# A paged-attention layer on one core: blocks exchanged directly from SBUF to SBUF, and new keys turned together with the first queries

## The chip, the core and the metric

The kernel runs on one core of a Trainium2 chip. The time is the device time of one execution in microseconds (us), as the median of several runs. The engines are TensorE (PE in the profile; its weight loads are listed as PEld), VectorE (DVE), ScalarE (ACT), GpSimd (POOL) and SyncE (SP), which here does nothing but issue transfers. Transfers are also issued from ScalarE's queue and from GpSimd's. All of them run on the core's 16 DMA engines.

## The reference

Eight sequences of 128 tokens with 512 features are first changed by a low-rank-adapter-like layer (one 512x512 matrix for each sequence, picked by a number), and then pass through one attention layer with a paged cache:

```python
x = x + einsum('bsi,boi->bso', x, weight[adapter_ids])
q, k, v = x @ Wq.T, x @ Wk.T, x @ Wv.T          # 32 query heads, 8 key heads of 128
q, k = rope(rmsnorm(q, q_norm_w), pos), rope(rmsnorm(k, k_norm_w), pos)
k_all = concatenate([k_cache[block_table], k])  # 512 cached keys, then 128 new ones
v_all = concatenate([v_cache[block_table], v])
scores = where(valid, q @ k_all.T / sqrt(128), -1e30)   # 4 query heads share a key head
x = x + (softmax(scores) @ v_all) @ Wo.T
```

Everything is float32.

## The kernel before, in words

The work is cut into 32 steps: four groups of key heads (two key heads and eight query heads each) times eight sequences. Step i works on the attention of its own group and sequence, on the projections of step i + 1, and on the value and output products of step i - 1. The steps 0 to 5 also compute the adapter layer of the later sequences.

A step has eight slots (h = 0 to 7), one for each block of scores: 128 rows by 640 keys. Four slots form a unit: the four query heads that share a key head (index j, 0 or 1), 32 tokens of each of the four heads in one slot. In a slot TensorE computes the scores (L1031), VectorE adds the mask and takes the minimum (L1041), ScalarE takes the exponential (L1057), VectorE the reciprocal of the sum (L1098), and GpSimd scales (L1105). Between two scores stand pieces of the other products (L559: `pj_kv`, `pj_q`, `o`, `out`), dealt out over the slots in the order of the list `main` so that each slot gets an equal share. The program writes out the order by hand; `pending`, `later`, `to_write` and `to_read` are lists of work that is emitted one slot later.

Three kinds of blocks have to be turned, with tokens or features brought onto the partitions: probabilities, cached keys and queries. VectorE turns them within blocks of 32 x 32 (`tp`, L871; `tk`, L786; `tq`, L807). What is left is an exchange of whole rows between partitions. The kernel before does this by way of DRAM, on SP's queue: one transfer writes the turned tile to a DRAM tile (`send`, `send_k`, `send_q`: L889, L791, L809), and a second one, which waits for the first, reads it back in the other order (`receive`, `receive_k`, `receive` in `send_q`: L898, L799, L816).

New keys (`k`, from the projection of step i + 1) are turned by TensorE instead: `turn_k` multiplies by the identity (L763) and ScalarE copies the result from PSUM into the last 128 columns of `kT` (L764). For that, `rotate` has GpSimd write the keys in a different order of their columns (`turned_order`, L671). `turn_k(i + 1, 0)` is placed in slot 6 of step i and `turn_k(i, 1)` in slot 2 of step i. At the ends of the program (the set `by_pe`: both query halves of step 0, the first of step 1, both of the last step) queries are turned by TensorE as well.

The weights of the next group are loaded, turned by VectorE, written to DRAM and read back in the same manner, on ScalarE's queue. Cached keys and values are gathered by GpSimd.

Buffers: `tk`, `tq0`, `tq1`, `kT0`, `kT1`, `qT0`, `qT1`, `q0`, `q1` and `k` have one buffer each, `tp` has two, `pT` one in each of two pools. The scores have two PSUM buffers, everything else four.

Of the kernel before, what the change touches and what calls it, by code (L numbers as in the profile page):

```python
# [18 lines left out]
P = 128  # L19
# [33 lines left out]
def lora_then_paged_attention(  # L53
# [173 lines left out]
    )  # L227
    mhalf = const.tile([P, GQ + GK], FP, name="mhalf")
    nc.gpsimd.memset(mhalf, -0.5)
    masks = [const.tile([P, 4, NC, Q4], FP, name=f"mask_{n}") for n in range(2)]  # L230
    for m in masks:
        nc.gpsimd.memset(m[:, :, LC, :], 0.0)


    lora_ix = const.tile([P, B], I32, name="lora_ix")
# [12 lines left out]

    steps = [(g, b) for g in range(G) for b in range(B)]
    last = len(steps) - 1  # L250
    TR = 0.11
    turns_at = {}

# [3 lines left out]
    for i, (g, b) in enumerate(steps):  # L257
        if i == 0:
            at(i, 2, False, lambda: turn_q(0, 1))
            at(i, 7, False, lambda: turn_q(1, 0))  # L260
            for n, h in enumerate((7, 8, 9, 10)):
                at(i, h, False, lambda n=n: turn_weights(("o1", 0, n)))
        if i == last:
            at(i - 1, 6, False, lambda: turn_q(last, 0))
            at(i, 2, True, lambda: turn_q(last, 1))
        at(i, 2, True, lambda i=i: turn_k(i, 1), 1)
        if i < last:
            at(i, 6, False, lambda i=i: turn_k(i + 1, 0), 1)
        if g == 0 and b + 2 < B:
            at(i, 0, True, lambda b=b: turn_x(b + 2))  # L270
            for c in range(KC):
                at(i, c if i else c + 2, False, lambda b=b, c=c: turn_lora(b + 2, c))
            at(i, 8 if i else 9, True, lambda b=b: turn_x1(b + 2))
    for turns in turns_at.values():
        turns.sort(key=lambda t: not t[0])

# [111 lines left out]
    def rope_angles():  # L388
        nc.vector.tensor_copy(row_f[:, 0:B], row_i[:, 0:B])
        row = spread(0)  # L390
        nc.vector.tensor_copy(len_f, row[:, 0:B])
        par_f = rope["par"] = const.tile([P, 1], FP, name="par_f")
        nc.vector.tensor_copy(par_f, par)
        pos = const.tile([P, B], FP, name="pos")
        nc.vector.tensor_scalar(pos, len_f, par_f, None, ALU.add)
        def temp(tag):
            t = work.tile([P, 4, D], FP, tag=tag, name=f"rope_{tag}")
            return t.rearrange("p h (u d) -> p (h u) d", u=2)
# [14 lines left out]
        nc.vector.tensor_scalar(ang, ang, PI_BELOW, -PI_BELOW, ALU.min, ALU.max)  # L413
        rope.update(ang=ang, sin=sin, cos=cos)
# [213 lines left out]

    def make_mask(i):

        b = steps[i][1]
        nc.vector.tensor_scalar(
            masks[i % 2][:, :, 0:LC, :], key_no, len_f[:, b : b + 1], FAR, ALU.is_ge, ALU.mult
        )


    by_pe = {(0, 0), (0, 1), (1, 0), (last, 0), (last, 1)}

    def rotate(i, y, dst, ss, table, n, between=None):

# [8 lines left out]
        sw = work.tile([P, 4, D], FP, tag="sw", name=f"sw_{i}_{table}")  # L649


        turned_order = i > 0 and (table == 1 or (i, n) in by_pe)
        cw = dst
        if turned_order and table:
            cw = sw[:, 2 : 2 + heads, :]
        elif turned_order:
            cw = work.tile([P, 4, D], FP, tag=f"tq{n}", name=f"cw_{i}_{n}")
# [46 lines left out]
    def project(i, what):  # L704
# [1 line left out]
        s = st[i]  # L706

        def after_kv(y):
            s.k = work.tile([P, GK, D], FP, tag="k", name=f"k_{i}")
            s.vn = news.tile([P, GW], FP, tag="vn", name=f"vn_{i}")  # L710
            s.ss = [
                small.tile([P, 6], FP, tag=f"ss{n}", name=f"ss_{i}_{n}") for n in range(2)
            ]

            def rest():
                nc.scalar.copy(s.vn, y[:, GW : 2 * GW])
                rotate(i, y, s.k, s.ss[0][:, 4:6], 1, 0)

            pending.append(rest)

        def after_q(n):
            def after(y):
                s.q[n] = work.tile([P, 4, D], FP, tag=f"q{n}", name=f"q_{i}_{n}")

                def rest():
                    rotate(
                        i,
                        y,
                        s.q[n],
                        s.ss[n][:, 0:4],  # L730
                        0,
                        n,
# [26 lines left out]
    def turn_k(i, j, copy=None):  # L759
# [3 lines left out]
        nc.tensor.transpose(t.rearrange("d i a -> d (i a)"), s.k[:, j, :], ident)  # L763
        (copy or nc.scalar.copy)(s.kT[j][:, :, LC, :].rearrange("d a i -> d i a"), t)  # L764

    def turn_q(i, n, copy=None):
        s = st[i]
        assert n in s.scaled
        s.qT[n] = work.tile([P, 4, 4, Q4], FP, tag=f"qT{n}", name=f"qT_{i}_{n}")
# [3 lines left out]
        (copy or nc.scalar.copy)(  # L773
            s.qT[n].rearrange("d b h q -> d h b q"), t.rearrange("d (h b q) -> d h b q", h=4, b=4)
        )


# [1 line left out]

    to_read = []  # L780

    def send_k(i):
        s = st[i]
        tk = work.tile([P, 4, GK, LC * Q4], FP, tag="tk", name=f"tk_{i}")
        for j in range(GK):
            nc.vector.transpose(  # L786
                tk[:, :, j, :].rearrange("p a (c k) -> p a c k", c=LC),
                s.kc[:, :, j * D : (j + 1) * D].rearrange("p c (a d) -> p a c d", a=4),
            )
        s.xk = xch.tile([4, P, GK, LC * Q4], FP, tag="xk", name=f"xk_{i}")  # L790
        nc.sync.dma_start(  # L791
            out=s.xk.rearrange("b (i a) h x -> (b i) (a h x)", a=4),
            in_=tk.rearrange("p a h x -> p (a h x)"),
        )

    def receive_k(i, j):
        s = st[i]
        s.kT[j] = work.tile([P, 4, NC, Q4], FP, tag=f"kT{j}", name=f"kT_{i}_{j}")
        nc.sync.dma_start(  # L799
            out=s.kT[j][:, :, 0:LC, :].rearrange("d b c k -> d b (c k)"),  # L800
            in_=s.xk[:, :, j, :].rearrange("b d x -> d b x"),
        )

    def send_q(i, n):
        s = st[i]
        tq = work.tile([P, 4, 4, Q4], FP, tag=f"tq{n}", name=f"tq_{i}_{n}")
        nc.vector.transpose(tq, s.q[n].rearrange("p h (a d) -> p a h d", a=4))  # L807
        xq = xch.tile([4, P, 4, Q4], FP, tag=f"xq{n}", name=f"xq_{i}_{n}")
        nc.sync.dma_start(  # L809
            out=xq.rearrange("b (i a) h q -> (b i) (a h q)", a=4),  # L810
            in_=tq.rearrange("p a h q -> p (a h q)"),
        )

        def receive():
            s.qT[n] = work.tile([P, 4, 4, Q4], FP, tag=f"qT{n}", name=f"qT_{i}_{n}")
            nc.sync.dma_start(  # L816
                out=s.qT[n].rearrange("d b h q -> d b (h q)"),
                in_=xq.rearrange("b d h q -> d b (h q)"),
            )

        to_read.append((now[0], 0, receive))

    now = [0]

# [59 lines left out]
            t[:, 0:LA].rearrange("p (c b q) -> p c b q", c=NC, b=4),  # L884
        )

    def send(u):
        u.scr = xch.tile([4, P, REP * QK], FP, tag="xp", name=f"xp_{u.i}_{u.j}")
        nc.sync.dma_start(  # L889
            out=u.scr.rearrange("b (i a) x -> (b i) (a x)", a=4),  # L890
            in_=u.tp.rearrange("p a r k -> p (a r k)"),
        )

    def receive(u):

        pl, tag = (lora, "raw") if u.j and u.i >= B - 3 else (pts, "pT")
        pT = pl.tile([P, 4, REP, QK], FP, tag=tag, name=f"pT_{u.i}_{u.j}")
        nc.sync.dma_start(  # L898
            out=pT.rearrange("p b r k -> p b (r k)"), in_=u.scr.rearrange("b p x -> p b x")
        )  # L900
        st[u.i].pT[u.j] = pT

    def run(queue):
# [77 lines left out]
    for i, (g, b) in enumerate(steps):  # L981
# [38 lines left out]
        for h in range(8):  # L1020
# [9 lines left out]
            for lo, hi in ((0, L), (L, LA)):  # L1030
                nc.tensor.matmul(  # L1031
                    sc[:, lo:hi],
                    lhsT=s.qT[j][:, r, :, :].rearrange("d h q -> d (h q)"),
                    rhs=s.kT[j].rearrange("d a c i -> d (a c i)")[:, lo:hi],
                    start=True,
                    stop=True,
# [4 lines left out]
            nc.vector.tensor_tensor_reduce(  # L1041
                out=p,
                in0=sc[:, 0:LA],
                in1=masks[i % 2].rearrange("p a c i -> p (a c i)"),
                scale=1.0,
                scalar=3.0e38,
                op0=ALU.add,
# [12 lines left out]
            if prev is not None:  # L1060
# [1 line left out]
                if u.i < last or u.j == 0:  # L1062
                    turn_p(u, pr)
                if pr == REP - 1:
                    send(u)
                    to_read.append((8 * i + h, 1, lambda u=u: receive(u)))
            run(later)
            run(to_write)
            if 8 * i + h in turn_when:
# [6 lines left out]
            for _, _, f in sorted(due, key=lambda r: r[1]):  # L1076
                f()
            if h == 0 and i:
                receive_k(i, 1)
            if h == (1 if i else 3) and i < last:  # L1080
                send_k(i + 1)
            if h == 4 and i < last:
                receive_k(i + 1, 0)

            ahead = sum(c for k in range(h + 1, 8) for _, c, _ in turns_at.get((i, k), []))
            mine = sum(t[1] for t in turns)
# [96 lines left out]
```

## Time and profile before

| what | value |
|---|---|
| time, median of 3 runs | 1198.78 us (1196.74 to 1199.55) |
| profiled execution, its own time | 1197.03 us |
| its span | 1194.7 us |
| PE busy | 1178.0 us, 99% |
| VectorE, ScalarE, GpSimd busy | 61%, 44%, 56% |
| DMA: SP's queue (q1), ScalarE's (q10), GpSimd's (q0), share of 16 engines | 59.6%, 12.4%, 10.1% |
| HBM read, written | 195.04 MB, 132.12 MB |
| length of a step, steps 1 to 5 / 8 to 28 | 40.7 us / 34.6 us |

The lines of the profile read as follows. A group names the line of the kernel, the engine and the operation, then the tiles as output<-input, the shape, the count, the busy time and the mean duration, and after the last bar how long the engine was idle just before and for whom. A wait line has the waiting engine and tile, whom it waited for, the total in us, how many times, and the longest. A line of transfers has the queue that issues it (SPq, ACTq, POOLq), how many there were, the size of one, and the median time in us from issue to landing. The chain of waits is the sequence of work that ended last. The rows of slices cut the span in 40 equal parts, and a digit is the busy share in tenths. Float32 products show as two records per matrix product, and a matmul's duration overlaps with that of its neighbour, so the spacing of starts is the price of one.

### The profile page before, as it was taken

Reading aid. Unit: us, or ns where it says so; the run is one execution under the profiler, and the core shown is the slowest. Engines: PE = TensorE matmul, PEld = TensorE weight load, DVE = VectorE, ACT = ScalarE, POOL = GpSimd, SP = SyncE. Lnnn points to the kernel's source line nnn. Section 1 sums busy time; section 2 is a strip of 40 time slices with the busy share of each in tenths; the row PEclk is TensorE's granted clock in tenths of the full one; section 3 lists DMA queues with packets and bytes.
Section 4 is the critical chain, followed back from the end, with each engine's and each line's share of the span. In section 5 each row is a group of like instructions: output and inputs, shape, how many; then the busy total and the mean of one; then the engine's idle time right before and its main releaser. Section 6 shows DMA issues by size and latency. Waiting matters only on the chain.

```text
span 1194.7 us, 12971 instructions
## 1 busy us (share of the span) xinstructions
PE 1178.0 (99%) x3412; PEld 576.4 (48%) x3412; DVE 733.6 (61%) x1675; ACT 531.5 (44%) x1648; POOL 674.9 (56%) x781
## 2 busy tenths in 40 slices
PE   7899999999999999999999999999999999999998
PEld 4554455454444444444444444444444444444454
DVE  5566656665566666766566676666657655565651
ACT  4564444444444444444444444444444444444432
POOL 5566455545566556555655556565556556655540
PEclk9999999999999999999999999999999999999999
DMA  8388788877988988888998998888898987777761
GB/s 290 110 278 273 261 292 293 275 261 246 309 289 301 334 303 300 294 270 300 296 303 280 340 313 298 298 278 300 267 319 277 303 285 264 243 255 242 260 222 60
DMA packets 187148, 328.02 MB, mean 275 GB/s; under 512 B 13124, under 2 KB 106052, under 8 KB 178116
## 3 DMA queue, kind: packets, MB, share of 16 engines
q1 hardware_dynamic: 124272, 239.23, 59.6%
q10 hardware_dynamic: 49524, 48.12, 12.4%
q0 software_dynamic: 13280, 39.86, 10.1%
q8 instruction: 27, 0.44, 0.2%
q14 instruction: 45, 0.37, 0.1%
HBM read 195.04 MB, written 132.12 MB: 274 GB/s over the span
## 4 chain that ended last, share of the span: by engine, by line
PE 97%; DMA 1%; ACT 1%; DVE 0%; POOL 0%; issue 0%; ACTq 0%; DVEq 0%; POOLq 0%
PE o L559 23%; PE sc L1031 23%; PE pj_q L559 18%; PE out L559 18%; PE pj_kv L559 9%; PE y L559 2%; PE lw L474 1%; DMA w_q<-xw_q 1%; PE x L474 1%; PE kt L763 1%; PE wt_q L492 0%; PE wt_kv L492 0%; PE qt L772 0%; PE wt_o L492 0%; PE pt L881 0%
## 5 line engine op out<-in xcount | busy, mean ns | idle before, releaser
L1041 DVE CUSTOM_DVE_ANT_0 p<-sc,mask 128x640 f32<-128x640 f32 x256 | 210.9, 824 | 400.5 <-PE sc L1031 400.4
L1057 ACT ACTIVATE p<-p,mn 128x640 f32<-128x640 f32 x256 | 211.6, 827 | 324.6 <-DVE mn L1041 322.4
L1031 PE MATMUL sc<-kT,qT 128*128 128x512 f32 (+1 forms) x1024 | 318.4, 433 | 1.1 <-ACT kT L764 0.8
L1105 POOL TENSOR_SCALAR p<-p,rc 128x640 f32<-128x640 f32 x252 | 201.9, 801 | 183.0 <-DVE rc L1098 181.0
L1031 PEld LDWEIGHTS sc<-kT,qT 128*128 128x128 f32 x1024 | 189.9, 190 | 226.4 <-issue 206.0
L559 PE MATMUL pj_q<-w_q,x1T 128*128 128x512 f32 x512 | 236.9, 593 | 1.4 <-ACT w_q L493 0.7
L559 PE MATMUL o<-pT,vc 128*128 128x512 f32 x512 | 236.9, 593 | 0.0
L559 PE MATMUL out<-w_o,oT 128*128 128x512 f32 (+1 forms) x528 | 234.9, 580 | 0.9 <-ACT oT L838 0.7
L871 DVE STREAM_TRANSPOSE tp<-p 128x640 f32<-128x640 f32 x252 | 211.0, 837 | 4.9 <-POOL p L1105 4.7
L610 POOL DMA_INDIRECT kc<-in_L_cond_k_cache_dram,key_ix x128 | 130.8, 1022 | 32.7 <-issue 32.5
L610 POOL DMA_INDIRECT vc<-in_L_cond_v_cache_dram,val_ix x128 | 127.9, 999 | 31.0 <-issue 30.8
L692 ACT ACTIVATE q<-q,rs 128x128 f32<-128x128 f32 x256 | 81.9, 390 | 139.1 <-POOL q L679 134.5
L559 PEld LDWEIGHTS out<-w_o,oT 128*128 128x128 f32 x528 | 95.7, 190 | 93.5 <-issue 89.9
L559 PEld LDWEIGHTS pj_q<-w_q,x1T 128*128 128x128 f32 x512 | 92.4, 190 | 93.8 <-issue 91.4
L559 PEld LDWEIGHTS o<-pT,vc 128*128 128x128 f32 x512 | 91.9, 190 | 88.6 <-issue 81.3
L559 PE MATMUL pj_kv<-w_kv,x1T 128*128 128x512 f32 x256 | 116.6, 593 | 0.7 <-ACT x1T L476 0.7
L671 POOL TENSOR_TENSOR k<-sw 128x256 f32<-128x256 f32 x31 | 22.9, 739 | 157.1 <-PE kt L763 133.4
L679 POOL TENSOR_TENSOR q<-q,sw 128x512 f32<-128x512 f32 x59 | 74.7, 1266 | 45.0 <-DVE sw L662 44.9
L646 ACT ACTIVATE sq<-pj_q 128x128 f32<-128x128 f32 x256 | 70.8, 277 | 50.4 <-PE pj_q L559 41.5
L687 POOL TENSOR_TENSOR rs<-ss,mhalf 128x6 f32<-128x6 f32 x64 | 77.6, 1212 | 5.3
L559 PEld LDWEIGHTS pj_kv<-w_kv,x1T 128*128 128x128 f32 x256 | 45.9, 190 | 45.6 <-issue 44.7
L559 PE MATMUL o<-pT,vn 128*128 128x512 f32 x128 | 65.4, 593 | 0.0
(123 smaller groups left out, 873.6 us busy)
## 6 DMA issues: line engine op xcount, KB each, us to landing
xp<-tp SPq DMA_DIRECT2D x63, 1280.0 KB, 5.9
pT<-xp SPq DMA_DIRECT2D x63, 1280.0 KB, 7.0
xk<-tk SPq DMA_DIRECT2D x31, 512.0 KB, 7.5
kT<-xk SPq DMA_DIRECT2D x62, 256.0 KB, 6.6
xq<-tq SPq DMA_DIRECT2D x59, 256.0 KB, 4.6
qT<-xq SPq DMA_DIRECT2D x59, 256.0 KB, 5.2
st_q<-in_L_cond_Wq_dram ACTq DMA_DIRECT2D x24, 256.0 KB, 5.3
xw_q<-tw_q ACTq DMA_DIRECT2D x24, 256.0 KB, 4.4
```

What stands on the lines that cost most here:

```text
L474: nc.tensor.transpose(t[:, j, :], blk, ident)
L559: nc.tensor.matmul(y[0], lhsT=lhsT, rhs=rhs, start=(k == 0), stop=(k == len(pieces) - 1))
L610: nc.gpsimd.indirect_dma_start(out=dst[:, c, :], out_offset=None, in_=src, in_offset=bass.IndirectOffsetOnAxis(ap=rows[:, g, at : at + 1], ...
L646: nc.scalar.activation(sq, t[:, h, :], AF.Square, scale=float(D) ** -0.5, accum_out=ss[:, h : h + 1])
L679: add.tensor_tensor(dst, cw, sw[:, 0:heads, :], ALU.add)
L687: nc.gpsimd.tensor_tensor(rs[:, 0:width], ss[:, 0:width], mhalf[:, 0:width], ALU.pow)
L692: nc.scalar.activation(q, q, AF.Identity, scale=rs[:, h : h + 1])
L871: nc.vector.transpose(u.tp[:, :, r, :], u.p.pop(r).rearrange("q (a k) -> q a k", a=4))
L1031: nc.tensor.matmul(sc[:, lo:hi], lhsT=s.qT[j][:, r, :, :].rearrange("d h q -> d (h q)"), rhs=s.kT[j].rearrange("d a c i -> d (a c i)")[:, ...
L1041: nc.vector.tensor_tensor_reduce(out=p, in0=sc[:, 0:LA], in1=masks[i % 2].rearrange("p a c i -> p (a c i)"), scale=1.0, scalar=3.0e38, op0 ...
L1057: nc.scalar.activation(p, p, AF.Exp, bias=unit.mn[:, one], scale=-1.0, accum_out=unit.sm[:, one])
L1105: nc.gpsimd.tensor_scalar(q, p, unit.rc[:, one], 1.0, ALU.mult, ALU.mult)
```

## The change

All exchanges on SP's queue lose their stop in DRAM. A new function issues four transfers, one for each block of 32 source partitions, straight from the turned tile to its destination in SBUF. `send` and `receive` are gone; `move` is emitted where `receive` was.

New keys are no longer turned by TensorE, except in steps with the first query half in `by_pe`. They lie behind the first query half in one tile (`q0` now has 4 + 2 blocks), are turned by VectorE and exchanged with them (`tq0` and `qT0` have six blocks), and ScalarE copies them from `qT0` into the last columns of `kT` (`copy_k`). For j = 0 this is placed in slot 7, ahead of the exponential, and for j = 1 in slot 2, as the turn was. Both are counted as no work for TensorE when the pieces are dealt out. `rotate` writes these keys in plain order.

The cached keys of the next step are turned in slot 2 instead of slot 1. There is one mask tile instead of two.

```diff
-    masks = [const.tile([P, 4, NC, Q4], FP, name=f"mask_{n}") for n in range(2)]
+    mask = const.tile([P, 4, NC, Q4], FP, name="mask")
...
-        at(i, 2, True, lambda i=i: turn_k(i, 1), 1)
-        if i < last:
-            at(i, 6, False, lambda i=i: turn_k(i + 1, 0), 1)
+        for j, n, slot in ((0, i - 1, 6), (1, i, 2)):
+            if (i, 0) in by_pe and i:
+                at(n, slot, bool(j), lambda i=i, j=j: turn_k(i, j), 1)
+            elif i:
+                at(n, slot + 1 - j, True, lambda i=i, j=j: copy_k(i, j), 0)
+            elif j:
+                at(n, slot, True, lambda: turn_k(0, 1), 1)
...
-        turned_order = i > 0 and (table == 1 or (i, n) in by_pe)
+        turned_order = i > 0 and (i, n) in by_pe
...
-            s.k = work.tile([P, GK, D], FP, tag="k", name=f"k_{i}")
+            s.q[0] = work.tile([P, 4 + GK, D], FP, tag="q0", name=f"q_{i}_0")
+            s.k = s.q[0][:, 4 : 4 + GK, :]
...
+    def copy_k(i, j):
+        s = st[i]
+        nc.scalar.copy(
+            s.kT[j][:, :, LC, :].rearrange("d a (b i) -> d a b i", b=4),
+            s.qT[0][:, :, 4 + j, :].rearrange("d b (i a) -> d a b i", a=4),
+        )
...
+    def exchange(dst, src):
+        for b in range(4):
+            nc.sync.dma_start(
+                out=dst[:, b, :].unsqueeze(1), in_=src[Q4 * b : Q4 * b + Q4, :, :]
+            )
...
     def send_k(i):
...
-        s.xk = xch.tile([4, P, GK, LC * Q4], FP, tag="xk", name=f"xk_{i}")
-        nc.sync.dma_start(
-            out=s.xk.rearrange("b (i a) h x -> (b i) (a h x)", a=4),
-            in_=tk.rearrange("p a h x -> p (a h x)"),
-        )
-    def receive_k(i, j):
+    def move_k(i, j):
         s = st[i]
         s.kT[j] = work.tile([P, 4, NC, Q4], FP, tag=f"kT{j}", name=f"kT_{i}_{j}")
-        nc.sync.dma_start(
-            out=s.kT[j][:, :, 0:LC, :].rearrange("d b c k -> d b (c k)"),
-            in_=s.xk[:, :, j, :].rearrange("b d x -> d b x"),
-        )
+        exchange(s.kT[j][:, :, 0:LC, :].rearrange("d b c k -> d b (c k)"), s.tk[:, :, j, :])
...
     def send_q(i, n):
         s = st[i]
-        tq = work.tile([P, 4, 4, Q4], FP, tag=f"tq{n}", name=f"tq_{i}_{n}")
+        heads = 4 if n else 4 + GK
+        tq = work.tile([P, 4, heads, Q4], FP, tag=f"tq{n}", name=f"tq_{i}_{n}")
         nc.vector.transpose(tq, s.q[n].rearrange("p h (a d) -> p a h d", a=4))
...
+        def move():
+            s.qT[n] = qT_tile(i, n)
+            exchange(
+                s.qT[n].rearrange("d b h q -> d b (h q)"), tq.rearrange("p a h q -> p a (h q)")
+            )
+        to_read.append((now[0], 0, move))
...
-    def send(u):
...
-    def receive(u):
+    def move(u):
         pl, tag = (lora, "raw") if u.j and u.i >= B - 3 else (pts, "pT")
         pT = pl.tile([P, 4, REP, QK], FP, tag=tag, name=f"pT_{u.i}_{u.j}")
-        nc.sync.dma_start(
-            out=pT.rearrange("p b r k -> p b (r k)"), in_=u.scr.rearrange("b p x -> p b x")
-        )
+        exchange(pT.rearrange("p b r k -> p b (r k)"), u.tp.rearrange("p a r k -> p a (r k)"))
...
                 if pr == REP - 1:
-                    send(u)
-                    to_read.append((8 * i + h, 1, lambda u=u: receive(u)))
+                    to_read.append((8 * i + h, 1, lambda u=u: move(u)))
...
             if h == 0 and i:
-                receive_k(i, 1)
-            if h == (1 if i else 3) and i < last:
+                move_k(i, 1)
+            if h == (2 if i else 3) and i < last:
                 send_k(i + 1)
             if h == 4 and i < last:
-                receive_k(i + 1, 0)
+                move_k(i + 1, 0)
```

More of the change, by code (lines that the diff above doesn't have):

```diff
@@ L229, in lora_then_paged_attention @@
     nc.gpsimd.memset(mhalf, -0.5)
-    masks = [const.tile([P, 4, NC, Q4], FP, name=f"mask_{n}") for n in range(2)]
-    for m in masks:
-        nc.gpsimd.memset(m[:, :, LC, :], 0.0)
+    mask = const.tile([P, 4, NC, Q4], FP, name="mask")
+    nc.gpsimd.memset(mask[:, :, LC, :], 0.0)
     lora_ix = const.tile([P, B], I32, name="lora_ix")
@@ L250, in lora_then_paged_attention @@
     last = len(steps) - 1
+    by_pe = {(0, 0), (0, 1), (1, 0), (last, 0), (last, 1)}
     TR = 0.11
@@ L396, in temp @@
         def temp(tag):
-            t = work.tile([P, 4, D], FP, tag=tag, name=f"rope_{tag}")
-            return t.rearrange("p h (u d) -> p (h u) d", u=2)
+            n = 4 + GK if tag in ("q0", "tq0") else 4
+            t = work.tile([P, n, D], FP, tag=tag, name=f"rope_{tag}")
+            return t[:, 0:4, :].rearrange("p h (u d) -> p (h u) d", u=2)
         ang, turns, sin, cos = temp("q0"), temp("q1"), temp("tq0"), temp("sw")
@@ L632, in make_mask @@
         nc.vector.tensor_scalar(
-            masks[i % 2][:, :, 0:LC, :], key_no, len_f[:, b : b + 1], FAR, ALU.is_ge, ALU.mult
+            mask[:, :, 0:LC, :], key_no, len_f[:, b : b + 1], FAR, ALU.is_ge, ALU.mult
         )
-    by_pe = {(0, 0), (0, 1), (1, 0), (last, 0), (last, 1)}
     def rotate(i, y, dst, ss, table, n, between=None):
@@ L656, in rotate @@
         elif turned_order:
-            cw = work.tile([P, 4, D], FP, tag=f"tq{n}", name=f"cw_{i}_{n}")
+            cw = work.tile([P, 4 if n else 4 + GK, D], FP, tag=f"tq{n}", name=f"cw_{i}_{n}")
+            cw = cw[:, 0:4, :]
         nc.vector.tensor_tensor(
@@ L722, in after @@
             def after(y):
-                s.q[n] = work.tile([P, 4, D], FP, tag=f"q{n}", name=f"q_{i}_{n}")
+                if n:
+                    s.q[n] = work.tile([P, 4, D], FP, tag=f"q{n}", name=f"q_{i}_{n}")
                 def rest():
@@ L728, in rest @@
                         y,
-                        s.q[n],
+                        s.q[n][:, 0:4, :],
                         s.ss[n][:, 0:4],
@@ L764, in turn_k, with qT_tile @@
         (copy or nc.scalar.copy)(s.kT[j][:, :, LC, :].rearrange("d a i -> d i a"), t)
+    def copy_k(i, j):
[4 more added lines that the diff above has]
+        )
+    def qT_tile(i, n):
+        heads = 4 if n else 4 + GK
+        return work.tile([P, 4, heads, Q4], FP, tag=f"qT{n}", name=f"qT_{i}_{n}")
     def turn_q(i, n, copy=None):
@@ L768, in turn_q @@
         assert n in s.scaled
-        s.qT[n] = work.tile([P, 4, 4, Q4], FP, tag=f"qT{n}", name=f"qT_{i}_{n}")
+        s.qT[n] = qT_tile(i, n)
         t = ps_mm.tile([P, HID], FP, tag="mm", name=f"qt_{i}_{n}")
@@ L773, in turn_q @@
         (copy or nc.scalar.copy)(
-            s.qT[n].rearrange("d b h q -> d h b q"), t.rearrange("d (h b q) -> d h b q", h=4, b=4)
+            s.qT[n][:, :, 0:4, :].rearrange("d b h q -> d h b q"), t.rearrange("d (h b q) -> d h b q", h=4, b=4)
         )
     to_read = []
+    def exchange(dst, src):
[3 more added lines that the diff above has]
+            )
     def send_k(i):
         s = st[i]
-        tk = work.tile([P, 4, GK, LC * Q4], FP, tag="tk", name=f"tk_{i}")
+        tk = s.tk = work.tile([P, 4, GK, LC * Q4], FP, tag="tk", name=f"tk_{i}")
         for j in range(GK):
@@ L789, in send_k @@
             )
-        s.xk = xch.tile([4, P, GK, LC * Q4], FP, tag="xk", name=f"xk_{i}")
-        nc.sync.dma_start(
-            out=s.xk.rearrange("b (i a) h x -> (b i) (a h x)", a=4),
-            in_=tk.rearrange("p a h x -> p (a h x)"),
-        )
-    def receive_k(i, j):
+    def move_k(i, j):
         s = st[i]
         s.kT[j] = work.tile([P, 4, NC, Q4], FP, tag=f"kT{j}", name=f"kT_{i}_{j}")
-        nc.sync.dma_start(
-            out=s.kT[j][:, :, 0:LC, :].rearrange("d b c k -> d b (c k)"),
-            in_=s.xk[:, :, j, :].rearrange("b d x -> d b x"),
-        )
+        exchange(s.kT[j][:, :, 0:LC, :].rearrange("d b c k -> d b (c k)"), s.tk[:, :, j, :])
     def send_q(i, n):
         s = st[i]
-        tq = work.tile([P, 4, 4, Q4], FP, tag=f"tq{n}", name=f"tq_{i}_{n}")
+        heads = 4 if n else 4 + GK
+        tq = work.tile([P, 4, heads, Q4], FP, tag=f"tq{n}", name=f"tq_{i}_{n}")
         nc.vector.transpose(tq, s.q[n].rearrange("p h (a d) -> p a h d", a=4))
[L808 to L811, printed above, removed]
-        )
[L814 to L818, printed above, removed]
+        def move():
+            s.qT[n] = qT_tile(i, n)
+            exchange(
+                s.qT[n].rearrange("d b h q -> d b (h q)"), tq.rearrange("p a h q -> p a (h q)")
             )
-        to_read.append((now[0], 0, receive))
+        to_read.append((now[0], 0, move))
     now = [0]
@@ L885, in turn_p_pe @@
         )
-    def send(u):
[L888 to L892, printed above, removed]
-    def receive(u):
+    def move(u):
         pl, tag = (lora, "raw") if u.j and u.i >= B - 3 else (pts, "pT")
         pT = pl.tile([P, 4, REP, QK], FP, tag=tag, name=f"pT_{u.i}_{u.j}")
-        nc.sync.dma_start(
-            out=pT.rearrange("p b r k -> p b (r k)"), in_=u.scr.rearrange("b p x -> p b x")
-        )
+        exchange(pT.rearrange("p b r k -> p b (r k)"), u.tp.rearrange("p a r k -> p a (r k)"))
         st[u.i].pT[u.j] = pT
@@ L1032, in lora_then_paged_attention @@
                     sc[:, lo:hi],
-                    lhsT=s.qT[j][:, r, :, :].rearrange("d h q -> d (h q)"),
+                    lhsT=s.qT[j][:, r, 0:4, :].rearrange("d h q -> d (h q)"),
                     rhs=s.kT[j].rearrange("d a c i -> d (a c i)")[:, lo:hi],
@@ L1043, in lora_then_paged_attention @@
                 in0=sc[:, 0:LA],
-                in1=masks[i % 2].rearrange("p a c i -> p (a c i)"),
+                in1=mask.rearrange("p a c i -> p (a c i)"),
                 scale=1.0,
```

## The prediction

> **What bounds the kernel now.** I read the page's busy table and its forty slices first.
>
> ```profile
> PE 1178.0 (99%) x3412; PEld 576.4 (48%) x3412; DVE 733.6 (61%) x1675; ACT 531.5 (44%) x1648; POOL 674.9 (56%) x781
> ...
> PE   7899999999999999999999999999999999999998
> ...
> PEclk9999999999999999999999999999999999999999
> DMA  8388788877988988888998998888898987777761
> ```
>
> TensorE has work in every slice at a full granted clock, and the DMA engines are also busy eight or nine tenths of the time. Busy matmuls overlap, so 99% alone proves little. Next I asked what TensorE waited for between 60 and 1150 us; this is the whole answer:
>
> ```profile
> PE pj_kv L559 <- ACT x1T L476: 0.7, 1, 0.7
> PE pj_q L559 <- issue: 0.5, 1, 0.5
> PE pj_q L559 <- DMA w_q<-xw_q: 0.2, 1, 0.2
> PE sc L1031 <- ACT qT L773: 0.2, 1, 0.2
> ```
>
> Those are 1.6 us of waiting in 1090 us. So transfers, VectorE, ScalarE and GpSimd are all hidden, and the period of a step is the sum of TensorE's own instructions. The chain of waits, around 499 and 519 us (start, length, what), gives their prices:
>
> ```profile
> 498.01 1.08 PE sc L1031 x4
> 499.09 0.11 PE kt L763
> 499.20 3.44 PE o L559 x8
> ...
> 516.40 2.58 PE out L559 x6
> 518.98 0.11 PE kt L763
> 519.09 1.08 PE sc L1031 x4
> ```
>
> A 512-column product takes 0.86 us (two records), a score 1.08, a turn of new keys (kt) 0.11. A late step has 30 products, 8 scores and 2 turns: 30 x 0.86 + 8 x 1.08 + 2 x 0.11 = 34.66 us; its starts are 34.6 us apart. Nothing is left over.
>
> **The change part by part.**
>
> *TensorE loses the turns of new keys.* The group is
>
> ```profile
> L763 PE MATMUL kt<-ident,k 128*128 128x128 f32 x64 | 17.4, 273 | 0.0
> ```
>
> The 273 ns overlaps with neighbours; the price on the path is the 0.108 us between two starts (0.11 in the chain). Six turns stay (steps 0, 1 and 31), 58 go: 58 x 0.108 = 6.3 us. This is the only edit that touches the bound. Otherwise TensorE keeps its instructions; in some steps one product moves across a score.
>
> *TensorE gains semaphore waits.* Each exchange is now four transfers with a semaphore each. The built program has 463 separate wait instructions on TensorE, the old one 282. In the trace one takes 51 ns, and two in a row start 111 ns apart under a 0.43 us matmul without a gap. The longest row is now three, in front of the first score of a unit: 0.12 + 2 x 0.111 + 0.051 = 0.39 us after the load before it, still ahead of the next load at 0.43. Cost 0; wholly exposed, 181 x 0.051 = 9.2 us.
>
> *VectorE* turns 128x768 instead of 128x512 for the first queries: 0.67 us x 1.5, so 0.33 more, 29 times, 10 us in all. VectorE waits 400 us for scores; cost 0. Cache keys are turned one slot later (h = 2), which sends that pair of 0.67 us turns past one score. Their GpSimd gathers at h = 3 start at 507.4 in the step shown, and the turns would end at about 504; nothing waits. One mask replaces two: it is written behind the last score of a step on the same engine, so there is no new wait.
>
> *ScalarE* copies 58 new-key blocks from SBUF instead of from PSUM. No row shows such a copy with 16-byte steps; the nearest is the old copy, 386 ns. I take 0; ends are -0.2 and +0.3 us each, hidden by 322 us that ScalarE waits for VectorE. But the copy now waits for the query exchange, ahead of the step's last exponential. GpSimd's add of keys loses its 133 us wait on kt, worth nothing since GpSimd is not the bound.
>
> *Transfers.* Each of 63 probability, 62 cache-key and 59 query exchanges changes from write-out plus read-back to four SBUF-to-SBUF transfers. The SP queue's transfers with their times to landing, and two issues in a step:
>
> ```profile
> xp<-tp SPq DMA_DIRECT2D x63, 1280.0 KB, 5.9
> pT<-xp SPq DMA_DIRECT2D x63, 1280.0 KB, 7.0
> xk<-tk SPq DMA_DIRECT2D x31, 512.0 KB, 7.5
> kT<-xk SPq DMA_DIRECT2D x62, 256.0 KB, 6.6
> xq<-tq SPq DMA_DIRECT2D x59, 256.0 KB, 4.6
> qT<-xq SPq DMA_DIRECT2D x59, 256.0 KB, 5.2
> ...
> 506.36 0.33 SPq L809 DMA_DIRECT2D xq<-tq  x1
> 510.31 0.37 SPq L816 DMA_DIRECT2D qT<-xq  x1
> ```
>
> The write-outs go: 114 MB in packets that held each of the 16 engines for about 226 (probabilities), 40 and 42 us, or 26% of the span. SP issues four times 0.36 us per exchange, six per step: 8.6 of 34.6 us. An SBUF-to-SBUF packet is nowhere in the trace. The row is the read-back: 2,560-byte packets at 102 ns, 32 per engine, 3.3 us for a probability exchange. [...] Each of the four transfers here reads 32 partitions. By the row the four pieces need 3.3 us, [...] No run here settles which; [...]
>
> *Is the data still in time?* First queries in a late step: turned by 506.3 (506.7 with keys), now issued by 508.2 rather than read back from 510.3; landed about 513.5 with the row's 5.2. The key copy stands before the exponential at 521.1, the next step's score at 523.6: cover 7 us or more, hence 0. Second queries, keys and probabilities have 6 us or more. In the first part (steps 1 to 5, period 40.7) it is closer: queries are turned 29 us into the step, SP issues them behind a probability exchange whose buffer comes free at about 28. By the row they land at 36 to 37, [...] the copy can go at 36 to 38 and the score is due at 40.7. So 0 by the row, [...] I take 0.3.
>
> *ScalarE's DMA queue.* The built order shows that a transfer waits for the one eight transfers earlier, from SP or ScalarE. With 766 instead of 367 on SP, eight back is now often in the slot before. Behind ScalarE's weight transfers stand squares, exponentials and copies of oT. Tightest is a step with a weight transfer after the fifth exponential, which ends 21.3 us into the step: it waits for a query piece issued at 18 to 19.3, landing at 23 to 24.5 by the row, so up to 3 us. Then come 1.9 us of squares. The scales they feed wait for GpSimd's add anyway, 3 us later, and the oT copy ends 2.2 us before the output product needs it. Cost 0; without that cover the cost is what the lateness exceeds 5 us by.
>
> *Sum.* -6.3 + 0.3 (first part) + 0.3 (start and end, where 13.6 us of TensorE idle may shift either way) = -5.7 us. The profiled execution took 1197.0 us (span 1194.7, 2.3 around it), so 1191.3; the median of the runs is 1.7 higher: 1193 us.
>
> **The rivals.** A difference under 0.2% (2.4 us) can't be told from none.
>
> *Late queries (no change).* [...] steps 1 to 5 lose about 1 us each: -6.3 + 5 = -1.3, 1197.5. [...] Against: the engines are emptier by a quarter, and kT can wait to 40.
>
> *ScalarE held by its queue (slower).* Place: a weight transfer in slots 4 or 5 of a step, holding the oT copy. Thirteen steps have one held by a query exchange of the slot before. It decides once these pieces land over 10 us after issue (19.3 + 10 = 29.3, then 1.3 us of scales and 0.6 of copy reach 31.2, when TensorE needs it). At 12 us each costs 2 to 2.5: 13 x 2.3 = 30, less 6, gives 1222; at 11, about 1209. For it: one ring order for all pieces, maximum landings of 10 to 11 us in the trace. Against: the typical 5.
>
> *Exposed waits (slower).* If the 181 waits cost their 51 ns, 9.2 - 6.3 = +2.9, 1201.7. Against: present pairs cost nothing.
>
> *More than the turns.* The few idle spots at projections and start close as transfers land sooner: up to 3 us more, 1190.
>
> *No effect of the turns.* Not likely: their 0.11 us is in the chain in each step.
>
> **How the numbers follow.** Turns alone: 0.60, own range 1191 to 1195.5. More: 0.08, faster. Late queries: 0.14, of which 0.05 is still faster by over 0.2%. Held queue: 0.13, slower by all but 0.01. Exposed waits: 0.05, 0.04 slower. Faster 0.60 + 0.08 + 0.05 = 0.73; slower 0.12 + 0.04 = 0.16; the rest, 0.11, within. The range runs from the larger gain, 1190, to 1202, which takes in exposed waits and late queries and leaves the held queue out.
>
> **What would show it.** kt 6 instead of 64 and steps of 34.4 us; TensorE still without waits after 60 us; the SP queue near 34% by the row [...]; written HBM bytes from 132 to about 18 MB. Wrong would be: TensorE waiting for oT or kT on ScalarE, with ScalarE idle behind its DMA issues (held queue); waits on the first score of a step before 280 us only (late queries); score loads starting late behind semaphores (exposed waits).

## The result, and the profile after

The changed kernel takes 1227.08 us (median of 4 runs, 1222.67 to 1230.02) against 1197.86 us (4 runs, 1196.74 to 1199.55): a ratio of 1.024, 95% interval 1.0205 to 1.0274. It is slower by 29 us, where 1193 us was forecast. The profiled execution has a span of 1225.2 us, 30.5 more than before.

The page of the changed kernel, busy table, slices, queues and HBM:

```profile
PE 1183.1 (97%) x3354; PEld 577.5 (47%) x3354; DVE 745.4 (61%) x1675; ACT 534.4 (44%) x1648; POOL 674.0 (55%) x780
...
PE   7898979889899999999999999999999999999998
...
PEclk9999989889999999999999999999999999999999
DMA  7376466565597797767797787766797776655642
...
q1 hardware_dynamic: 111072, 128.76, 45.5%
...
HBM read 80.74 MB, written 17.83 MB: 80 GB/s over the span
```

The 58 turns are gone (3354 matmuls instead of 3412), the traffic of HBM fell as forecast, and the DMA engines have more room on average. All the harm is in the first third: there the row of TensorE has eights and sevens, and the row of its clock has eights. The waits of TensorE between 60 and 1150 us, with the key copy's own waits:

```profile
PE sc L1037 <- ACT kT L778: 25.8, 5, 6.6
...
ACT kT L778 <- DMA kT<-tk: 34.8, 4, 11.0
...
ACT kT L778 <- DMA qT<-tq: 9.0, 1, 9.0
```

Five waits, one at the first score of each of the steps 2 to 6, each for the key copy (L778), which itself waits for a transfer. The copy reads `qT0`, so what it needs is the query exchange (L832, by way of L806); the trace names the transfer that landed nearest to it, sometimes that of the cached keys. The chain of waits in front of the second of these scores has both:

```profile
158.07 8.78 DMA qT<-tq
...
166.87 3.67 DMA kT<-tk
170.54 0.41 ACT kT L778
...
171.00 2.50 PE sc L1037 x4
```

In windows cut at these scores (length; busy time of TensorE, of its weight loads, of VectorE, ScalarE and GpSimd; granted clock, DMA share, GB/s), with one stretch of late steps:

```profile
121.00:171.00 50.00, 43.15 (x124) 21.68 (x125) 25.93 (x53) 18.98 (x57) 21.43 (x24) 0.91 0.61 167
171.00:220.00 49.00, 42.44 (x125) 21.25 (x125) 26.66 (x54) 18.61 (x56) 21.61 (x24) 0.95 0.59 157
...
267.00:314.00 47.00, 43.64 (x124) 21.90 (x124) 24.73 (x52) 18.36 (x55) 20.67 (x23) 0.93 0.57 145
...
500.00:600.00 100.00, 100.00 (x268) 47.13 (x267) 68.39 (x153) 44.85 (x140) 59.98 (x67) 1.00 0.71 187
```

The same stretch before, from the score at 116 us to the next step's:

```profile
116.00:157.00 41.00, 41.00 (x128) 20.43 (x128) 25.56 (x53) 18.59 (x55) 21.70 (x25) 1.00 0.83 283
```

From the first score of step 1 to that of step 6 it takes 240.4 us instead of 204.9: 35.5 more. TensorE idles 26.4 us between 60 and 350 us (1.1 before); the other 10 us are work at a granted clock of 0.91 to 0.95. (Before the change step 1 is 42.1 us long and steps 2 to 5 are 40.7.) Steps 8 to 28 are 34.4 us instead of 34.6, without a wait, as the sum had it. So the gain of 6 us is there, and 36 us are lost ahead of it.

Where the wait begins can be read off SP's queue in step 1, which is the first that suffers (start, length of four issues together, transfer). After:

```profile
103.85 4.98 SPq L806 DMA_DIRECT2D pT<-tp  x4
108.94 4.72 SPq L806 DMA_DIRECT2D qT<-tq  x4
113.71 0.60 SPq L104 DMA_DIRECT2D acc<-in_x_dram  x1
114.43 3.23 SPq L806 DMA_DIRECT2D kT<-tk  x4
```

Before, for the same three tiles:

```profile
104.80 0.37 SPq L898 DMA_DIRECT2D pT<-xp  x1
107.16 0.37 SPq L816 DMA_DIRECT2D qT<-xq  x1
107.59 0.50 SPq L104 DMA_DIRECT2D acc<-in_x_dram  x1
```

The probability exchange is issued at the same point, but it holds SP for 4.98 us instead of 0.37. Its four issues last 0.54, 0.60, 1.97 and 1.73 us: the third and fourth last about as long as a piece takes to move at the rate found below (327,680 bytes at 185 GB/s are 1.77 us). Everything behind it on SP is issued later: the last query piece at 113.1 instead of 107.2, the next x at 113.7 instead of 107.6.

### The profile page after: what moved, and what is told of

It reads as the page before. It is cut to its first block, busy times and chain, and to the rows that moved or that the text cites. A ratio compares the mean times of both kernels' runs of the same rounds, so it can differ in the third digit from the quotient of the medians.

```text
span 1225.2 us, 13384 instructions
## 1 busy us (share of the span) xinstructions
PE 1183.1 (97%) x3354; PEld 577.5 (47%) x3354; DVE 745.4 (61%) x1675; ACT 534.4 (44%) x1648; POOL 674.0 (55%) x780
## 3 DMA queue, kind: packets, MB, share of 16 engines
q1 hardware_dynamic: 111072, 128.76, 45.5%
## 4 chain that ended last, share of the span: by engine, by line
PE 92%; DMA 4%; ACT 1%; SPq 1%; DVE 1%; issue 1%; POOL 0%; ACTq 0%; DVEq 0%; POOLq 0%
PE sc L1037 23%; PE o L566 23%; PE pj_q L566 18%; PE out L566 15%; PE pj_kv L566 9%; DMA qT<-tq 3%; PE y L566 2%; PE lw L481 1%; DMA kT<-tk 1%; PE x L481 1%; SPq L806 1%; DVE p L1047 0%; PE wt_q L499 0%; PE wt_kv L499 0%; PE qt L793 0%
## 5 line engine op out<-in xcount | busy, mean ns | idle before, releaser
L1037 PE MATMUL sc<-kT,qT 128*128 128x512 f32 (+1 forms) x1024 | 324.7, 440 | 26.8 <-ACT kT L778 25.8
L1037 PEld LDWEIGHTS sc<-kT,qT 128*128 128x128 f32 x1024 | 194.2, 193 | 262.2 <-issue 226.9
L685 POOL TENSOR_TENSOR q<-q,sw 128x512 f32<-128x512 f32 (+1 forms) x89 | 96.8, 1087 | 98.8 <-DVE sw L668 98.6
L566 PEld LDWEIGHTS pj_kv<-w_kv,x1T 128*128 128x128 f32 x256 | 46.0, 190 | 45.6 <-issue 44.7
L1103 DVE RECIPROCAL rc<-sm 128x1 f32<-128x1 f32 x256 | 33.4, 130 | 46.0 <-ACT p L1063 46.0
```

Source lines behind the costliest of these rows:

```text
L566: nc.tensor.matmul(y[0], lhsT=lhsT, rhs=rhs, start=(k == 0), stop=(k == len(pieces) - 1))
L685: add.tensor_tensor(dst, cw, sw[:, 0:heads, :], ALU.add)
L1037: nc.tensor.matmul(sc[:, lo:hi], lhsT=s.qT[j][:, r, 0:4, :].rearrange("d h q -> d (h q)"), rhs=s.kT[j].rearrange("d a c i -> d (a c i)")[: ...
L1103: nc.vector.reciprocal(unit.rc[:, one], unit.sm[:, one])
```

## Three theories

Q, the order: queries stand behind a probability exchange that waits for its only buffer. P, the exchange itself: read 32 partitions at a time it is too slow, and so holds whatever is behind it. K, the copy: the key copy in front of a step's last exponential on ScalarE is what costs. The rates below come from the packet records of the trace: for each probability exchange of 512 packets of 2,560 bytes, the middle 410 packets over the time in which they started, and of these the median over the exchanges that start between 75 and 320 us. The waits are TensorE's idle time between 60 and 350 us, in gaps over 0.25 us. Each ratio below is to the kernel before, run again beside the kernel in question.

## Experiments on the order and the copy

**Queries first.** In steps 1 to 5 the first unit's probabilities are exchanged a slot later:

```diff
-                    to_read.append((8 * i + h, 1, lambda u=u: move(u)))
+                    held = 1 if 0 < i <= 5 and u.j == 0 else 0
+                    to_read.append((8 * i + h + held, 1, lambda u=u: move(u)))
...
-            to_read[:] = [r for r in to_read if r[0] == 8 * i + h]
+            to_read[:] = [r for r in to_read if r[0] >= 8 * i + h]
```

> The changed kernel, but in steps 1 to 5 the probability exchange of a step's first unit is issued on SP one slot later, behind the first queries' exchange. Theory Q (the queries are late because they stand behind a probability exchange that waits for its one buffer): steps 1 to 5 come back from 47-50 us to 41-42 us, waits of TensorE for kT at a step's first score vanish, time 1193 to 1196. Theory P (the four pieces are too slow in themselves, by issue and by rate): the probabilities now land late instead, 2 to 3 us a step stay lost, about 1205 to 1210. Theory K (the key copy in front of the last exponential on ScalarE is the cost): copy and wait stay, about 1227.

Measured: 1219.2 us, ratio 1.018 (1.012 to 1.023). No theory had this. The wait for keys is gone, and another stands in its place; the waits of TensorE and SP's queue in step 3:

```profile
PE x L481 <- DMA acc<-in_x_dram: 17.0, 4, 6.3
```

```profile
199.05 2.49 SPq L806 DMA_DIRECT2D qT<-tq  x4
201.70 7.17 SPq L806 DMA_DIRECT2D pT<-tp  x4
208.92 1.60 SPq L104 DMA_DIRECT2D acc<-in_x_dram  x1
```

Now the load of the next x is issued 9.9 us after the queries, because 7.17 us of probability pieces stand before it, and TensorE waits for x. Q is half right: the order decides who pays. It doesn't make the cost.

**Queries and x first.** The edit above, and `load_x(b + 3)` moved from slot 6 to slot 3.

```diff
-            if g == 0 and h == 6 and b + 3 < B:
+            if g == 0 and h == 3 and b + 3 < B:
                 load_x(b + 3)
+            if g == 0 and h == 6 and b + 3 < B:
                 gather_lora(b + 3)
```

> As the run with the queries first in steps 1 to 5, with the load of the next x issued three slots earlier too, ahead of the probability exchange. If the slow exchange blocks whatever stands behind it on SP, the wait moves on again: TensorE no longer waits for x, now the key exchange of the next step, issued 40 to 43 us into the step, is 1 to 4 us late; 1198 to 1208. If queries and x were the only transfers without slack: 1191 to 1195.

Measured: 1214.8 us, ratio 1.014 (1.011 to 1.017). The wait moved on again, but not to the keys, as I had expected:

```profile
PE o L566 <- DMA qT<-tq: 5.7, 1, 5.7
PE o L566 <- DMA xw_q<-tw_q: 5.6, 1, 5.6
PE lw L481 <- DMA lraw<-in_L_cond_weight_dram,lora_ix: 5.0, 2, 3.6
```

The value products (`o`) and the adapter matrix of the next sequence are late. In the first of these waits, at 164 to 170 us, the packets of the probability exchange run from 155 to 169 us, with the gathers of values and of the 1 MB adapter matrix and a weight transfer beside them; so most likely the probabilities themselves are what is late. The releasers that the lines name are the transfers that ended nearest. Three placements, three victims, and 16 to 29 us of loss against the kernel before in each: this speaks for P.

**Probabilities by HBM.** `send` and `receive` as before the change; queries and keys direct.

> The changed kernel, but probabilities go through HBM as before the change (write-out and read-back); queries and keys stay direct, keys turned by VectorE. Q and P both say that the probability exchange in front of the queries is the cost: steps 1 to 5 at 41 to 42 us, time 1192 to 1196. K: the loss stays, about 1227.

Measured: 1203.3 us (20 runs, 1198.0 to 1211.3), ratio 1.0038 (1.0022 to 1.0055). In the profile steps 2 to 5 are 40.5 us, as Q and P wanted, and no key copy is waited for more than 0.3 us; K falls by that. But the time is 7 us over the expected range. In the profiled execution the first score is 2 us later than in the changed kernel's (TensorE's clock is recorded as full only from 16.2 us on, and there from 10.4), step 1 is 44.0 us, and

```profile
PE pj_q L566 <- DMA w_q<-xw_q: 5.2, 2, 2.6
```

two weight tiles on ScalarE's queue come late, at 602 and 880 us. ScalarE's queue is the place of the rival *ScalarE held by its queue*, whose price was 30 us. Why it shows in this mix and not in the changed kernel I didn't find out.

**Keys by TensorE.** `turn_k` in every step again, queries exchanged alone.

> The changed kernel, but TensorE turns the new keys in every step as before the change; the direct exchanges stay, the query exchange then carries queries alone (4 heads instead of 6 in the first of a step). K: stalls gone, about 1197. Q and P: the queries are as late as they were, a score waits for qT instead of kT; loss stays but for a third less data in that exchange, 1229 to 1234 (58 turns of 0.108 us come back).

Measured: 1222.9 us, ratio 1.019 (1.015 to 1.023). The key copy is gone, and 25 us of the loss are still there, now as `PE x L481 <- DMA acc<-in_x_dram` (15.7 us, 4 times). K falls as the cause: the copy was only the first that came late. The time is also 6 us below what Q and P said, since they took over the old waits unchanged, and with the smaller query exchange (256 KB instead of 384) step 1 has none: it is 42.1 us there instead of 47.3.

## Experiments on the rate

**All partitions at a time.** The same four transfers with the same packets, each read from all 128 partitions, so that other rows arrive than those of the exchange:

```diff
-                out=dst[:, b, :].unsqueeze(1), in_=src[Q4 * b : Q4 * b + Q4, :, :]
+                out=dst[:, b, :].unsqueeze(1), in_=src[:, b, :].unsqueeze(1)
```

> The changed kernel, but each of the four pieces of an exchange reads all 128 partitions of its source instead of 32 of them: same number of transfers, same packets and bytes, other rows, so what the scores and values get is not the reference's data. P by rate [...]: the probability exchange of steps 1 to 5 goes from 7 us to about 4, the stalls at a step's first score shrink from 4-7 us to 1-3, time about 1205 to 1210. If the rate is set by something else (issue on SP, competition of other transfers): no change, about 1227.

Measured: 1190.3 us, ratio 0.992 (0.989 to 0.995): the whole loss is gone and the whole gain stays, more than P had claimed. Of its page, and of SP's queue in step 1:

```profile
PEclk9999999999999999999999999999999999999999
...
q1 hardware_dynamic: 111072, 128.76, 30.9%
```

```profile
104.00 2.42 SPq L806 DMA_DIRECT2D pT<-tp  x4
106.53 2.81 SPq L806 DMA_DIRECT2D qT<-tq  x4
109.38 0.59 SPq L104 DMA_DIRECT2D acc<-in_x_dram  x1
```

As many packets and bytes as in the changed kernel hold the engines for 30.9% of the span instead of 45.5%. The rate is 388 GB/s instead of 185. Four issues still cost 2.42 us, so an issue of a piece is about 0.60 us even when nothing backs up, and that is harmless here. What hurts is that the pieces are slow, and it hurts twice. In step 1 of the changed kernel the last query piece has left SP 39.5 us after the step's first score and the last query packet goes at 46.1; here it is 35.1 and 37.6. So about half of the lateness is there when SP has issued the queries, and half comes after that.

**Which partitions.** Two kernels read 64 partitions and two rows of each; once all from one half, once across the middle:

```diff
-                out=dst[:, b, :].unsqueeze(1), in_=src[Q4 * b : Q4 * b + Q4, :, :]
+                out=dst[:, b, :].unsqueeze(1),
+                in_=src[64 * (b // 2) : 64 * (b // 2) + 64, 2 * (b % 2) : 2 * (b % 2) + 2, :],
```

> The changed kernel, but each of the four pieces reads 64 partitions (the first two pieces 0 to 63, the other two 64 to 127) and two rows of each instead of 32 partitions and four rows: same bytes, packets and transfers, other rows, so the data that scores and values get is not the reference's. Theory H [...]: 64 partitions of one half are no faster than 32, [...] time as the changed kernel's, 1220 to 1230. Theory N (the rate goes with the number of partitions read): twice the rate, time 1190 to 1200.

```diff
+                in_=src[32:96, 2 * (b % 2) : 2 * (b % 2) + 2, :],
```

> The changed kernel, but each piece reads partitions 32 to 95 and two rows of each: again 64 partitions, half of them on each side of 64, and again data that is not the reference's. H [...] rate as with all 128 partitions, time 1189 to 1192. N (number of partitions): the same as the piece of partitions 0 to 63 gives, whatever that is.

Measured: 1205.5 us from one half (ratio 1.0063, 1.0039 to 1.0087), 1192.5 us across (0.9958, 0.9944 to 0.9972). The number of partitions is the same, the rate is 205 GB/s and 311 GB/s. So it isn't the number alone that decides (theory N), but also on which side of 64 they lie (theory H). Neither theory is exact: 64 partitions of one half are 11% faster than 32 and cost 22 us less than they do, which is more than H allowed, and 64 across reach 311, not the 388 of all 128.

**Order of the pieces.** `for b in (0, 2, 1, 3)`:

> The changed kernel, with the four pieces of each exchange issued in the order 0, 2, 1, 3, so that neighbours in the queue read opposite halves of the partitions. If the DMA engines overlap neighbouring pieces, [...] the probability exchange goes from 7 us towards 4, and the time falls to 1195 to 1215. If each engine finishes a piece before the next, no change: 1222 to 1230.

Measured: 1217.9 us, ratio 1.015 (1.012 to 1.018), 224 GB/s; between the two expectations. The order alone brings 39 GB/s, too little.

**Two queues.** The probabilities' last two pieces go by ScalarE's queue:

```diff
-            nc.sync.dma_start(
+            (nc.sync if b < 2 else odd or nc.sync).dma_start(
...
-        exchange(pT.rearrange("p b r k -> p b (r k)"), u.tp.rearrange("p a r k -> p a (r k)"))
+        exchange(pT.rearrange("p b r k -> p b (r k)"), u.tp.rearrange("p a r k -> p a (r k)"), nc.scalar)
```

> The changed kernel, with the last two pieces of each probability exchange (partitions 64 to 127) issued from ScalarE's queue instead of SP's, so that both halves of the partitions can be read at the same time. By H the probability exchange goes from 7 us towards 4 and SP is held for 1.2 us instead of 5 us: the waits of steps 1 to 5 shrink; but ScalarE waits in its program order until the probabilities' buffer is free. If that wait is short, 1191 to 1200; if it holds the exponentials, 1205 to 1240.

Measured: 1204.5 us, ratio 1.0042 (1.0023 to 1.0061); between the two expectations. The rate is 236 GB/s.

```profile
109.55 1.19 SPq L806 DMA_DIRECT2D pT<-tp  x2
110.85 6.61 SPq L806 DMA_DIRECT2D qT<-tq  x4
```

```profile
PE sc L1037 <- ACT kT L778: 6.4, 5, 2.1
```

SP is rid of the probabilities after 1.19 us, but the query pieces then stand for 6.61 us. TensorE waits 6.4 us at first scores instead of 25.8, at most 2.1 at a time, and twice (2.9 us) for a copy of oT that ScalarE makes late.

The packet records show how the late queries and the length of a step hang together. For step 1 of each kernel, in us after its first score: the probability exchange's first and last packet, the last packet of the query exchange behind it, and the length of the step.

| pieces | GB/s | probabilities, first to last | last query packet | step 1 | idle of TensorE, 60 to 350 us |
|---|---|---|---|---|---|
| 32 partitions (the change) | 185 | 30.9 to 39.2 | 46.1 | 47.3 | 26.4 |
| 32, order 0, 2, 1, 3 | 224 | 30.9 to 39.8 | 44.2 | 45.3 | 16.1 |
| 64 of one half | 205 | 30.9 to 37.6 | 41.2 | 42.2 | 8.9 |
| 32, two queues | 236 | 31.9 to 39.4 | 42.5 | 43.6 | 8.3 |
| 64 across | 311 | 31.4 to 36.3 | 39.0 | 42.4 | 0.9 |
| all 128 | 388 | 30.8 to 34.4 | 37.6 | 42.0 | 0.7 |

In the three rows where the last query packet goes after 42 us, the step ends 1.1 to 1.2 us behind it (the copy of 0.41 us and what stands around it); where it goes by 41.2, the step has about its own length, 42.0 to 42.4. The rate alone doesn't order the rows: in step 1 one half at 205 GB/s beats two others at 224 and 236. In the 32-partition kernels the slowest tenth of the 2,560-byte packets takes 0.39 us or more while the median stays at 0.10; in the one-half kernel it takes 0.22 or more, with a median of 0.19. A query exchange is complete only with its slowest packets: in step 1 of the changed kernel 453 of its 512 packets have started by 41 us, and the last 59 take until 46.1. Why these packets are late the trace doesn't show.

A part of the times of these kernels has nothing to do with the exchanges. TensorE's clock is recorded as full from 10.4 us on in the changed kernel's trace, from 16.2 with 64 partitions across, and from 22.4 and 22.6 with two queues and with the order 0, 2, 1, 3. The same eight records of the first `y` product last 3.67 us in the changed kernel and 6.02 in the last one. The first score stands at 40.8, 42.9, 45.5 and 45.6 us accordingly. So two of these traces can differ by 4.8 us before step 0 begins, and the columns of the table, which leave this start out, compare better than the total times. Why the clock comes up at different times is open; no exchange has been issued by then.

## Experiments towards a better kernel

**Direct exchanges without the first part.** Probabilities of steps 1 to 5 go by HBM, everything else as changed:

```diff
+        if 0 < u.i <= 5:
+            nc.sync.dma_start(
+                out=pT.rearrange("p b r k -> p b (r k)"), in_=u.scr.rearrange("b p x -> p b x")
+            )
+        else:
+            exchange(pT.rearrange("p b r k -> p b (r k)"), u.tp.rearrange("p a r k -> p a (r k)"))
...
+                    if 0 < u.i <= 5:
+                        send(u)
```

> The changed kernel, but the probabilities of steps 1 to 5 go through HBM as before the change; later steps and all queries and keys stay direct. If the whole loss is the slow probability exchange ahead of queries and loads in the first part: steps 1 to 5 at 40.5 to 40.7 us, later ones at 34.4, no wait of TensorE between; 1197.8 - 58 x 0.108 = 1191.5, so 1190 to 1193, faster than both kernels. If direct queries and keys are late there even so: 1195 to 1205.

Measured: 1191.2 us (6 runs, 1189.7 to 1194.8), ratio 0.9947 (0.9930 to 0.9964): faster than both kernels. SP's queue in step 1, and two rows of the page:

```profile
104.24 0.38 SPq L914 DMA_DIRECT2D pT<-xp  x1
104.72 2.57 SPq L806 DMA_DIRECT2D qT<-tq  x4
107.35 0.70 SPq L104 DMA_DIRECT2D acc<-in_x_dram  x1
```

```profile
PE   7899999999999999999999999999999999999998
...
PEclk9999999999999999999999999999999999999999
```

With 0.38 us of issue in place of 4.98, the load of x is issued at 107.4 us again, and the last query packets land 36 to 40 us into the steps. The whole loss comes from the direct probability exchange in these five steps.

**The turns alone.** All exchanges by HBM as before the change; VectorE turns the new keys, and ScalarE lays them in place:

> The changed kernel with all three exchanges written out to HBM and read back as before the change; the part that stays is that VectorE turns the new keys with the first queries and ScalarE lays them in place. If the gain of the turns is independent of how data is moved: 58 x 0.108 us less than before in every step, steps of 34.4 us, 1191 to 1193, the same as with direct exchanges after step 5 (1191.2). If the direct exchanges bring something of their own in the late steps, or the larger query exchange (384 KB by HBM) is late: 1194 to 1200.

Measured: 1193.8 us (7 runs, 1193.0 to 1195.8), ratio 0.9951 (0.9934 to 0.9968). The turns give the gain; nearly nothing is left for the direct exchanges, even where they do no harm. The interval overlaps that of the run above; these two don't tell whether the direct exchanges of the late steps bring 2 us or nothing. In the traces, steps 8 to 30 take 790.4 us before the change, 785.0 in the changed kernel, 786.2 in the run above and 787.7 here, and 2.6 us of that last number are waits of TensorE; for the largest, 1.7 us, the profile shows no releaser.

## Why the prediction was wrong

*TensorE loses the turns of new keys*, -6.3 us: right. kt is at 6, late steps at 34.4 us, and the two kernels without a slow exchange in the first part come out at 1191.2 and 1193.8 us, where the sum had 1193.

*TensorE gains semaphore waits*, 0: right. In the late steps the chain runs on without a gap.

```profile
509.69 1.72 PE o L566 x4
511.41 1.08 PE sc L1037 x4
512.49 2.58 PE o L566 x6
515.07 0.86 PE out L566 x2
```

*VectorE*, *ScalarE*, 0: no run speaks against them. VectorE waits 384 us for scores in the changed kernel. Its wider turn takes 0.93 us, 0.26 more than before where I had 0.33, and ScalarE's new copy 0.41 us against 0.39.

*Transfers*: this step failed first. I took the row of 102 ns a packet, from transfers that read DRAM, and wrote that no run settled it. The runs do, against the row: 185 GB/s, and 8.3 us for the probability exchange of step 1 where the row gave 3.3. The median packet took 102 ns here too, which shows why that row was no measure of the rate: the mean went to 192 ns (108 with all partitions). The issue was also mis-sized. I took 0.36 us four times from a row of transfers that read DRAM; a piece costs 0.54 at least and about 0.60 when nothing backs up, and in step 1 the third and fourth, with two pieces ahead of them, cost 1.97 and 1.73. An exchange of probabilities thus holds SP for 5 us, not for 1.4. SP's queue takes 45.5% of the engines' time, well over the sign I had named for the row (34%).

*Is the data still in time?*: this is the term that made the sign wrong. Its mechanism, queries late behind the probabilities in steps 1 to 5, is the one that happened, and only there. By the row it was to cost nothing, and it was 4 to 7 us of waiting a step. For step 1 I had the queries landing at 36 to 37 by the row, and what went into that was short. The probabilities' buffer lets SP issue at 29.7 us, not at 28, and their first packet goes at 30.9. They take 8.3 us, not 3.3, with gathers and loads beside them. And the queries behind them run to 46.1 us, 6.9 us past the last probability packet. Then comes a cost that had no term in the sum: the work after each of the five waits goes on at a granted clock of 0.50 for 3.0 to 5.9 us, and 10 us more are lost there. The 0.3 in the sum leaned on the row; the 1 us a step of the rival *Late queries*, 5 us in all, was my estimate, with no measured number of this case behind it, and it was not the far end.

Of the rivals, *Late queries* named the place and the cause, and its sign, waits on the first score of a step in the first part only, is what the trace shows (to 315 us, not to 280); it put the time at 1197.5 us, 30 us short. It counted the lateness of one exchange and neither SP's standing still nor the lower clock, nor the next victim (x, then probabilities), which the first two experiments show to be waiting in line. *Exposed waits* and *More than the turns* left no trace. *ScalarE held by its queue* did not happen in the changed kernel; small pieces of it show in two other mixes (5.2 us for `w_q`, 2.9 us for `oT`).

## What to carry to other kernels

A transfer is not priced by the median of its packets: here that was 102 ns before and after, and the rate 185 GB/s from 32 partitions and 388 from all. Ask which partitions it reads at one time, and take the slow price when the row at hand comes from a transfer that reached all of them. Then ask how long the queue stands behind it: here a slow exchange of 4.98 us on SP put off all that SP issued after it (the next x from 107.6 to 113.7 us), so list all of that, with its slack, and not just the first. Where a stage has little slack and another has much, change the second alone: here the stage with 7 us of slack (an estimate from the trace before) took the same exchange at no cost, with steps of 34.4 us and no wait.

## What the runs showed of the hardware

- Pieces of 327,680 bytes from 32 partitions moved at 185 GB/s, from 64 of one half of the partitions at 205, from 64 across the middle at 311, from 128 at 388; destinations and packets were the same.
- The issue of such a piece took SP 0.54 us at least in the changed kernel (0.46 with all partitions). The median was 0.91 us for the pieces of probabilities, which back up, and 0.60 for those of keys and queries, against 0.36 to 0.40 for a read-back of the whole exchange from HBM. In step 1 of the changed kernel the third and fourth piece of the probabilities took 1.97 and 1.73 us, about as long as a piece takes to move at 185 GB/s (1.77 us), and the first two of the queries behind them 1.46 and 1.92.
- The granted clock fell to 0.50 in the five steps of the changed kernel in which TensorE waited several microseconds. Around each of the five waits of 3.7 to 6.6 us the trace has one stretch at 0.50, four of 6.8 us and one of 3.4, which begins 2.8 to 5.3 us after TensorE went idle. The second one, and the rest of its step:

```profile
171.00:174.20 3.20, 3.20 (x9) 2.16 (x10) 0.83 (x2) 1.94 (x6) 1.90 (x2) 0.50 0.00 1
174.20:218.00 43.80, 39.10 (x117) 18.94 (x115) 25.84 (x53) 16.07 (x48) 19.72 (x22) 1.00 0.64 170
```

The score at 171.0 us took 2.50 us instead of 1.08. Behind the waits 3.0 to 5.9 us of each stretch remain, 22.6 in all, and half of that, 11 us, is lost (an estimate from these stretches, 1.5 of it in step 6); that agrees with the 10 us found above. By these stretches a wait lost 2.3 us beyond itself (an estimate: half of 22.6 us, over five waits). Shorter waits were followed by such stretches too: in the run with the queries first, one of 2.1 us by 3.4 us at 0.50, and in the one-half run waits of 2.3 and 2.5 us by 6.8 and 3.4. In the run with two queues, whose waits were at most 2.1 us, the clock stayed at 1.00 from 22.4 us to the end. I put nothing for this loss, since I had expected no such wait.
